# Channel attention in a four-layer model: buffers cleared in front, GpSimd in written order, keys split from queries and made a batch earlier

## The chip, the core and the metric

The kernel runs on one core of one Trainium2 chip. The metric is device time in microseconds (us) of one execution; lower is better. Engines are called as the profile calls them: PE (TensorE matmuls), PEld (its weight loads), DVE (VectorE), ACT (ScalarE), POOL (GpSimd) and SP (SyncE, which here only issues DMAs). "L1567" is line 1567 of the kernel before the change.

## The reference

The model has four layers, each with an attention over a context and a feed-forward part, both gated by a `tanh`. The activations `x` are 16 batches of 128 x 256 in f32, the context `c` likewise. The change concerns the attention of the last layer, which runs over channels: the 128 rows are 16 heads of 8 channels, and the 256 columns are the positions.

```python
q = jnp.einsum('oc,bct->bot', Wq, x) + bq[None, :, None]      # x is layernormed over its columns
k = jnp.einsum('oc,bct->bot', Wk, c) + bk[None, :, None]
v = jnp.einsum('oc,bct->bot', Wv, c) + bv[None, :, None]
q, k, v = (t.reshape(B, 16, 8, -1) for t in (q, k, v))
scores = jnp.einsum('bhkt,bhks->bhts', q, k) * SCALE
p = jax.nn.softmax(scores, axis=-1)
out = jnp.einsum('bhts,bhks->bhkt', p, v).reshape(B, 128, T)
return jnp.einsum('oc,bct->bot', Wo, out) + bo[None, :, None]
# and around it:  x = x + tanh(g) * attention(layernorm(x), c)
```

Ahead of it stands a mixture of experts, whose rows lie sorted in DRAM (`ys`); its sum into `x` is made by this stage. After it comes a last feed-forward stage.

## The kernel before, in words

The whole pass is one program; the stage in question is `stage_l3x`. It runs without the search for row maxima (`search` is false in the pass that is timed; a second pass with `search` runs only if a flag demands it).

**The work of one batch `b`.** `begin` fetches the two expert rows of every token with two indirect DMAs issued by POOL (`fetch`, L709, tile `yc`, three buffers) and loads the context (`cb`) through SP. `stats` adds the two rows into `x` with their weights (L1524), takes mean and variance (L1527 to L1530). `rsqrt` raises the variance to -0.5 on POOL (L1535). `normal` writes the normalised queries `xn` on DVE (L1541). `project` makes queries (L1553, from `xn`) and keys (L1554, from `cb`) in one PSUM tile `qk`; `biased` adds the biases on DVE (tile `f`, L1559 and L1560). `halves` splits `f` into a rounded half (ACT, L1566) and the rest (POOL, L1567) in one tile `hl` for queries and keys together, and SP writes them in four DMAs to a DRAM scratch `scr` (L1571, L1573), one scratch per buffer set. `spread` reads the scratch back in four DMAs (L1589) into `qa` and `ka`, where a head has its rows on the partitions that the score matmuls want. `project_v` and `keep_v` make the values in `v`.

**Scores and products.** The loop runs over units `n = 8 b + u`. In each unit `weigh` makes one score group of four matmuls on PE (`s`, L1660, two PSUM buffers) and one exponential on ACT (`pt`, L1667). Two units feed one value product of 16 matmuls (`values`, `av`, L1676), which DVE copies out (`keep_values`, `avs`, L1687). When the four products of a batch are there, `back` transposes them (`ta`, L1692), `normalise` divides, `turn` transposes again (`tt`), `output` projects (`y`), `store` scales on ACT (`ys`, L1723) and adds to `x` on POOL (L1725).

**What sets the order.** PE, DVE and ACT are under a manual schedule: they execute in the order in which the code writes the instructions. That order is two tables: `taken[u]` lists what is written before score group `u`, `made[u]` what is written after it, each with the number of batches it runs ahead. POOL and SP are ordered by the framework's scheduler, which placed eight gathers at the head of POOL's stage and from then on a pair after each `hl`. There are three sets of `qa`, `ka` and `v` (`NB = 3`); `clear` sets a set to zero when its first batch comes: `qa` on DVE (L1546), `ka` and `v` on ACT (L1548), and a column of `v` to one on POOL (L1549).

Of the kernel before, what the change touches and what calls it, by code (L numbers as in the profile page):

```python
# [10 lines left out]
F32 = mybir.dt.float32  # L11
BF16 = mybir.dt.bfloat16
F32R = mybir.dt.float32r
AF = mybir.ActivationFunctionType
ALU = mybir.AluOpType
# [3 lines left out]
P = 128  # L19
B = 16  # L20
D = 256
# [34 lines left out]
def passage(ctx: ExitStack, tc: tile.TileContext, a: dict, out: bass.AP, inv, flag):  # L56
    nc = tc.nc
    search = inv is None
# [60 lines left out]
    ones = cst.tile([P, P], F32, name="ones")  # L119
# [46 lines left out]
    def bc(ap, axis, n):  # L166

        u = ap.unsqueeze(axis)
        shape = list(u.shape)
        shape[axis] = n  # L170
        return u.to_broadcast(shape)
# [1306 lines left out]
    def stage_l3x(wn, bn, wv, won, bov, pos, wgt, ys):  # L1478
# [5 lines left out]
        SC = float(1.0 / np.sqrt(8))  # L1484
        LEAD = 12
        NB = 4 if search else 3
        with tc.tile_pool(name="l3", bufs=1) as l3, tc.tile_pool(name="l3w", bufs=2) as w_, tc.tile_pool(
            name="l3d", bufs=1, space=bass.MemoryType.DRAM
# [3 lines left out]
            engines={mybir.EngineType.PE, mybir.EngineType.DVE, mybir.EngineType.Activation}  # L1492
# [3 lines left out]
            scr = [l3d.tile([8, P, D], F32, name=f"scr{i}") for i in range(NB)]  # L1496
            zr = l3.tile([2, P], F32, name="zr")
# [6 lines left out]
            def begin(b):  # L1504
                fetch(b)
                cbs[b] = w_.tile([P, D], F32, name="cb", bufs=3 if search else 4)
                nc.sync.dma_start(cbs[b], a["ctx"][b])
# [43 lines left out]
            def project(b):  # L1551
                ps["f", b] = t = psa.tile([P, 2, D], F32, name="qk", tag="a")
                nc.tensor.matmul(t[:, 0, :], lhsT=wn[0], rhs=xns.pop(b), start=True, stop=True)  # L1553
                nc.tensor.matmul(t[:, 1, :], lhsT=wn[1], rhs=cbs[b], start=True, stop=True)  # L1554

            def biased(b):
                t = ps.pop(("f", b))
                fs[b] = f = w_.tile([P, 2, D], F32, name="f")
                nc.vector.tensor_scalar(f[:, 0, :], t[:, 0, :], bn[0], SC, ALU.add, ALU.mult)  # L1559
                nc.vector.tensor_scalar(f[:, 1, :], t[:, 1, :], bn[1], None, ALU.add)  # L1560

            def halves(b):

                f = fs.pop(b)
                hl = w_.tile([P, 2, 2, D], F32R, name="hl")
                nc.scalar.copy(hl[:, :, 0, :], f)  # L1566
                nc.gpsimd.tensor_tensor(hl[:, :, 1, :], f, hl[:, :, 0, :].bitcast(F32), ALU.subtract)  # L1567
                s = scr[b % NB]
                hf = hl.bitcast(F32)
                for x in range(2):  # L1570
                    nc.sync.dma_start(s[2 * x : 2 * x + 2].rearrange("s p t -> p s t"), bc(hf[:, 0, x], 1, 2))  # L1571
                for x in range(2):
                    nc.sync.dma_start(s[4 + 2 * x : 6 + 2 * x].rearrange("s p t -> p s t"), hf[:, 1])  # L1573

            def spread(b):

                s = scr[b % NB]
                for h in range(2):
                    r = slice(64 * h + 32, 64 * h + 34)
                    if not search:  # L1580
                        continue
                    if b < NB:
                        nc.sync.dma_start(kas[b][r].bitcast(F32), bc(ones[0:2, :], 1, 16))
                    else:
                        nc.sync.dma_start(qas[b % NB][r].bitcast(F32), bc(zr, 1, 16))
                s = s.rearrange("s (k h) t -> (s k) (h t)", h=16)
                for h in range(2):
                    for x, t in enumerate((qas, kas)):
                        nc.sync.dma_start(  # L1589
                            t[b % NB][64 * h : 64 * h + 32].bitcast(F32).rearrange("p j t -> p (j t)"),  # L1590
                            s[32 * x : 32 * x + 32, 2048 * h : 2048 * h + 2048],
                        )
# [140 lines left out]
            if search:  # L1733
# [3 lines left out]
                    ((keep_values, -1, 3), (biased, 4)),  # L1737
                    ((normalise, -1, 0), (halves, 4), (keep_v, 3)),
# [7 lines left out]
                    ((values, -1, 3), (project, 4)),  # L1746
# [5 lines left out]
                    ((values, 0, 2), (output, -1), (spread, 4)),  # L1752
                )
            else:
                taken = (
                    ((begin, 4), (rsqrt, 3), (keep_values, -1, 2), (spread, 2)),
                    ((normal, 3), (clear, 3)),
                    ((keep_values, -1, 3),),
                    ((normalise, -1, 0), (normalise, -1, 1), (biased, 3)),
                    ((keep_values, 0, 0), (halves, 3)),  # L1760
# [5 lines left out]
                    (),  # L1766
                    ((values, -1, 3),),
                    ((back, -1, 0), (back, -1, 1), (project, 3)),
# [5 lines left out]
                )  # L1774
            for n in range(-40, 8 * B + 17):
                b, u = divmod(n, 8)
                for f, d, *r in taken[u]:
                    when(f, b + d, *r)
                if search and 0 <= n + LEAD < 8 * B:
                    top(n + LEAD)  # L1780
                if 0 <= n < 8 * B:
                    weigh(n)
                for f, d, *r in made[u]:
                    when(f, b + d, *r)
# [280 lines left out]
```

## Time and profile before

| | |
|---|---|
| median of 3 runs | 1079.16 us (1078.13 to 1082.75) |
| the profiled execution | 1077.04 us, of which span 1075.3 us |
| busy in the span | PE 904.1, PEld 602.5, DVE 607.5, ACT 456.8, POOL 342.3 us |
| the stage `stage_l3x` | from about 752 us (first clear on ACT at 752.50) to about 970 us of the span |
| first score group of the stage | 786.87 us |
| last score matmul starts | 968.7 us |
| score groups, `s`, L1660 | 512 matmuls, 64.3 us busy |
| exponentials, `pt`, L1667 | 128 instructions of 1024 ns |
| value products, `av`, L1676 | 1024 matmuls, 69.4 us busy |
| halves on POOL, `hl`, L1567 | 16 instructions of 1282 ns |

The page's busy times are sums over stages with different limits. Times in the stage are counted from the start of the span. A bracket at the end of a line of the timeline tells how long the engine stood idle before the line, and what it is thought to have waited for.

### The profile page before, as it was taken

The page shows a single profiled execution, that of the slowest core. Times are in us where ns is not written, and L with a number is a line of the kernel's source. Part 1 is how long each engine was busy: PE and PEld are TensorE (multiplying, and loading weights), DVE is VectorE, ACT ScalarE, POOL GpSimd, SP SyncE. Part 2 cuts the span into 40 slices and gives each one's busy share as a digit, 9 for nine tenths or more (in the row PEclk, how much of TensorE's full clock was granted, in tenths as well). Part 3 has the DMA queues.
Part 4 walks back from the last instruction along what each step waited for, and adds up shares of the span by engine and source line. Part 5 has one row for each costly group of instructions (what it writes and reads, how often), then busy time and mean ns, then how long its engine had stood idle before and what let it go on. Part 6 is the DMA issues. An engine that isn't in the chain of part 4 may idle for free. (4 is left out here: it accounts for less than half of the span.)

```text
span 1075.3 us, 14892 instructions
## 1 busy us (share of the span) xinstructions
PE 904.1 (84%) x5212; PEld 602.5 (56%) x5212; DVE 607.5 (56%) x1537; ACT 456.8 (42%) x707; POOL 342.3 (32%) x389
## 2 busy tenths in 40 slices
PE   3899978899999888888864858998169999998797
PEld 1444456677778444455443747887145555555564
DVE  5988966322225656787788586454345555534442
ACT  1211024223322446666762242454257777882111
POOL 5766322543115324211111046550443342201000
PEclk9999979999999978999986557899579999997999
DMA  9100070233341109800000202352488887530000
GB/s 305 41 1 1 0 220 21 63 104 109 69 143 50 39 20 144 78 1 1 1 1 1 78 1 88 109 145 82 142 247 235 220 222 195 164 79 1 20 30 32
DMA packets 71401, 94.12 MB, mean 88 GB/s; under 512 B 9271, under 2 KB 63127, under 8 KB 69015
## 3 DMA queue, kind: packets, MB, share of 16 engines
q1 hardware_dynamic: 56952, 67.21, 21.1%
q0 software_dynamic: 14080, 23.78, 11.4%
q10 hardware_dynamic: 288, 2.10, 0.5%
q8 instruction: 45, 0.74, 0.3%
q14 instruction: 36, 0.29, 0.1%
HBM read 57.06 MB, written 33.55 MB: 84 GB/s over the span
## 5 line engine op out<-in xcount | busy, mean ns | idle before, releaser
L1667 ACT ACTIVATE pt<-s 128x1024 f32<-128x1024 f32 x128 | 126.4, 1024 | 32.5 <-PE s L1660 29.8
L709 POOL DMA_INDIRECT yc<-ys,pos x64 | 62.4, 975 | 125.0 <-DVE x L729 49.2
L297 PE MATMUL y<-kv,toep 128*128 128x512 f32 x192 | 86.6, 602 | 1.6 <-DVE toep L237 1.6
L1660 PE MATMUL s<-qa,ka 64*128 64x256 f32 x512 | 64.3, 332 | 8.3 <-ACT pt L1667 7.5
L1676 PE MATMUL av<-pt,v 128*32 128x256 f32 x1024 | 69.4, 389 | 0.1
L289 POOL TENSOR_TENSOR kv<-ctxT 128x1024 f32<-128x1024 f32 x32 | 60.2, 1900 | 28.3 <-PE y L297 28.3
L1660 PEld LDWEIGHTS s<-qa,ka 64*128 64x128 f32 x512 | 38.6, 188 | 46.9 <-issue 23.2
L1687 DVE COPY avs<-av 128x256 f32<-128x256 f32 x64 | 27.1, 423 | 65.5 <-PE av L1676 48.5
L297 PEld LDWEIGHTS y<-kv,toep 128*128 128x128 f32 x192 | 35.6, 192 | 43.7 <-issue 40.3
L616 PE MATMUL ub<-L0we,xbT 128*128 x160 | 50.8, 460 | 2.6 <-ACT xbT L607 2.6
L593 POOL DMA_INDIRECT xb<-xs,who x40 | 38.2, 954 | 43.3 <-PE tb L605 33.2
L913 PE MATMUL yb<-L2we,hT 88*128 (+1 forms) x224 | 41.7, 315 | 9.6 <-DVE hT L737 3.9
L848 POOL DMA_INDIRECT xb<-xs,who x40 | 38.1, 953 | 31.7 <-PE tb L860 20.9
L302 DVE TENSOR_TENSOR pr<-y,qT 128x1024 f32<-128x1024 f32 x32 | 39.0, 1222 | 12.1 <-PE y L297 9.4
L1567 POOL TENSOR_TENSOR hl<-f,hl 128x512 fp32r<-128x512 f32 x16 | 20.5, 1282 | 79.5 <-ACT hl L1566 79.5
L477 PE MATMUL up<-L0s,xT 128*128 128x352 f32 x128 | 43.0, 482 | 0.0
L913 PEld LDWEIGHTS yb<-L2we,hT 88*128 88x128 f32 x224 | 33.6, 205 | 16.5 <-DVE hT L737 9.0
L1086 PE MATMUL s<-qa,ka 18*128 18x512 f32 x128 | 37.4, 660 | 4.9 <-ACT follow L1380 4.9
L305 DVE TENSOR_REDUCE oT<-pr 128x128 f32<-128x1024 f32 x32 | 38.9, 1219 | 1.0
L1676 PEld LDWEIGHTS av<-pt,v 128*32 128x32 f32 x1024 | 26.9, 110 | 20.4 <-issue 0.7
L642 PE MATMUL yb<-L0we,hTb 88*128 x160 | 37.9, 379 | 0.0
L616 PEld LDWEIGHTS ub<-L0we,xbT 128*128 128x128 f32 x160 | 28.8, 190 | 15.5 <-ACT xbT L607 2.8
(384 smaller groups left out, 2043.1 us busy)
## 6 DMA issues: line engine op xcount, KB each, us to landing
scr<-hl SPq DMA_DIRECT2D x64, 256.0 KB
ys<-ysb SPq DMA_DIRECT2D x40, 256.0 KB
qa<-scr SPq DMA_DIRECT2D x32, 256.0 KB
ka<-scr SPq DMA_DIRECT2D x32, 256.0 KB
L2we<-in_L_w_dram POOLq DMA_DIRECT2D x6, 792.0 KB
L0we<-in_L_w_dram SPq DMA_DIRECT2D x6, 704.0 KB
xs<-xn SPq DMA_DIRECT2D x8, 512.0 KB
x<-in_x_dram SPq DMA_DIRECT2D x4, 512.0 KB
```

Of the source, the lines that this page charges most:

```text
L289: nc.gpsimd.tensor_tensor(t, bc(ch, 3, 8), bc(ch, 2, 8), ALU.mult)
L297: nc.tensor.matmul(y[:, ns], lhsT=T[:, h, d : d + P], rhs=kv[mc][:, ns], start=(mc == 0), stop=(mc == lc))
L302: nc.vector.tensor_tensor(pr, y.rearrange("p (b j i) -> p b j i", b=B, j=8), bc(qT[:, lc, :, hs], 2, 8), ALU.mult)
L305: nc.vector.tensor_reduce(oT[:, lc, :, hs], pr, AX.X, ALU.add)
L477: nc.tensor.matmul(t[:, n, 0 : 2 * I], lhsT=xT[:, c, b * P : (b + 1) * P], rhs=s13[:, c, n, :], start=(c == 0), stop=(c == 1),)
L593: nc.gpsimd.indirect_dma_start(out=xbs[s][:, i, :], out_offset=None, in_=xs, in_offset=bass.IndirectOffsetOnAxis(ap=who[:, 2 * s + i : 2 * ...
L616: nc.tensor.matmul(t[:, i, 0 : 2 * I], lhsT=xbT[:, i, c, :], rhs=we[:, bass.ds(regs[s][i] + c * 2 * I, 2 * I)], start=(c == 0), stop=(c == 1),
L709: nc.gpsimd.indirect_dma_start(out=got[b][:, i, :], out_offset=None, in_=ys, in_offset=bass.IndirectOffsetOnAxis(ap=pos[:, i, b : b + 1], ...
L913: nc.tensor.matmul(y[:, i, :], lhsT=hT[:, x, k, i, :], rhs=we[0:HI, bass.ds(at[i] + 4 * I + k * D, D)], start=(n == 0), stop=(n == 3),)
L1660: nc.tensor.matmul(s[:, h, jj, :], lhsT=ka[r, 2 * i + jj, sc * P : (sc + 1) * P], rhs=qa[r, 2 * i + jj, :], start=True, stop=True,)
L1667: nc.scalar.activation(pts[b, i][:, sc], s, AF.Exp)
L1676: nc.tensor.matmul(av[c : c + 32, :], lhsT=va[:, sc, 8 * h + 2 * i + jj, :], rhs=pt[:, sc, h, jj, :], start=(sc == 0), stop=(sc == 1),)
```

## The change

It does four things in `stage_l3x`, all for the pass without search as far as order goes.

1. POOL joins the manual schedule of the stage, so its instructions stand in written order.
2. All three sets of buffers are cleared before the loop, not one by one in it.
3. `project`, `biased`, `halves` and `spread` take queries (`x = 0`) and keys (`x = 1`) separately, with tiles of half the size: `qk` and `f` hold one of them, `hl` has four buffers of half size. The number of scratches is `NB + 1 = 4`.
4. Keys are projected, split and written to scratch a batch earlier than queries. The keys of the first three batches are also spread at once (`ahead`); those of later batches are spread with the queries of the same batch (`behind`). The context is loaded five batches ahead; the gathers (`fetch`, four ahead) now stand after the `rsqrt` of their unit.

```diff
-            engines={mybir.EngineType.PE, mybir.EngineType.DVE, mybir.EngineType.Activation}
+            engines={
+                mybir.EngineType.PE, mybir.EngineType.DVE,
+                mybir.EngineType.Activation, mybir.EngineType.Pool,
+            }
...
-            scr = [l3d.tile([8, P, D], F32, name=f"scr{i}") for i in range(NB)]
+            NS3 = NB + 1
+            scr = [l3d.tile([8, P, D], F32, name=f"scr{i}") for i in range(NS3)]
...
+            def project(b, x):
+                ps["f", b, x] = t = psa.tile([P, D], F32, name="qk", tag="a")
+                nc.tensor.matmul(t, lhsT=wn[x], rhs=cbs[b] if x else xns.pop(b), start=True, stop=True)
...
+            def halves(b, x):
+                f = fs.pop((b, x))
+                hl = w_.tile([P, 2, D], F32R, name="hl", bufs=4)
+                nc.scalar.copy(hl[:, 0, :], f)
+                nc.gpsimd.tensor_tensor(hl[:, 1, :], f, hl[:, 0, :].bitcast(F32), ALU.subtract)
+                s = scr[b % NS3]
+                hf = hl.bitcast(F32)
+                for i in range(2):
+                    at = 4 * x + 2 * i
+                    nc.sync.dma_start(
+                        s[at : at + 2].rearrange("s p t -> p s t"), hf if x else bc(hf[:, i], 1, 2)
+                    )
...
+            def ahead(b):
+                if b < NB:
+                    spread(b, 1)
+
+            def behind(b):
+                if b >= NB:
+                    spread(b, 1)
+                spread(b, 0)
...
                 taken = (
-                    ((begin, 4), (rsqrt, 3), (keep_values, -1, 2), (spread, 2)),
-                    ((normal, 3), (clear, 3)),
-                    ((keep_values, -1, 3),),
-                    ((normalise, -1, 0), (normalise, -1, 1), (biased, 3)),
-                    ((keep_values, 0, 0), (halves, 3)),
+                    ((context, 5), (rsqrt, 3), (fetch, 4), (keep_values, -1, 2), (behind, 2)),
+                    ((normal, 3), (biased, 4, 1)),
+                    ((keep_values, -1, 3), (halves, 4, 1)),
+                    ((normalise, -1, 0), (normalise, -1, 1), (biased, 3, 0), (ahead, 4)),
+                    ((keep_values, 0, 0), (halves, 3, 0)),
...
                 made = (
-                    (),
+                    ((project, 4, 1),),
                     ((values, -1, 3),),
-                    ((back, -1, 0), (back, -1, 1), (project, 3)),
+                    ((back, -1, 0), (back, -1, 1), (project, 3, 0)),
...
+                for b in range(NB):
+                    clear(b)
             for n in range(-40, 8 * B + 17):
```

## The prediction

> **What bounds the kernel now.** I read the table by stretches first, over the channel attention (752 to 970 us of the span); columns are span, then busy us and instructions of PE, PEld, DVE, ACT and POOL, then granted clock, DMA share and GB/s.
>
> ```profile
> 752.00:770.00 18.00, 2.04 (x4) 1.17 (x4) 4.91 (x10) 3.38 (x4) 8.55 (x11) 0.50 0.35 102
> 770.00:787.00 17.00, 5.92 (x18) 4.68 (x18) 9.19 (x19) 6.98 (x7) 7.86 (x10) 0.50 0.75 216
> 787.00:798.00 11.00, 6.70 (x44) 3.92 (x44) 3.42 (x10) 6.56 (x8) 4.72 (x5) 0.67 0.87 241
> ...
> 813.20:824.90 11.70, 11.14 (x120) 6.58 (x116) 6.45 (x22) 9.06 (x12) 4.51 (x6) 1.00 0.98 289
> ...
> 907.05:918.18 11.13, 11.07 (x122) 6.58 (x118) 6.33 (x22) 9.18 (x12) 2.54 (x4) 1.00 0.75 202
> ```
>
> There are two regimes. Up to 798 no engine is full: PE works 14.7 of 46 us, at half clock. This is the ramp, a chain of waits. After it PE is busy 11.1 of every 11.1 to 11.7 us: a plateau that PE bounds. The ramp's waits come next (total us, times, longest):
>
> ```profile
> PE qk L1553 <- DVE xn L1541: 28.8, 4, 15.0
> DVE xn L1541 <- POOL rs L1535: 10.0, 3, 3.3
> ```
>
> PE waits for the normalised queries, and those wait for GpSimd's power. GpSimd's timeline says why:
>
> ```profile
> 756.03 0.95 POOL L709 DMA_INDIRECT yc<-ys,pos  x1 [3.83 <-ACT v L1548]
> ...
> 764.80 0.95 POOL L709 DMA_INDIRECT yc<-ys,pos  x1 [0.30 <-issue]
> 765.77 0.60 POOL L1535 TENSOR_TENSOR rs<-ve,neghalf 128x1 f32<-128x1 f32 x1
> 770.65 1.27 POOL L1567 TENSOR_TENSOR hl<-f,hl 128x512 fp32r<-128x512 f32 x1 [4.28 <-ACT hl L1566]
> 772.08 1.00 POOL L709 DMA_INDIRECT yc<-ys,pos  x1 [0.16 <-issue]
> 773.39 0.95 POOL L709 DMA_INDIRECT yc<-ys,pos  x1 [0.30 <-issue]
> 774.36 0.59 POOL L1535 TENSOR_TENSOR rs<-ve,neghalf 128x1 f32<-128x1 f32 x1
> ```
>
> The variance of batch 0 was ready at 761.77, but eight gathers stood ahead of the power: 4.0 us lost. Later powers stand behind two gathers each. DVE writes xn at 766.40, 774.99, 783.54 and 792.18, about 8.6 us apart; the fourth is the last obstacle, because the projection of batch 3 stands in PE's order before score group 3 of batch 0 (794.65), and from there the plateau runs.
>
> The plateau itself changes pace: 11.73 us a batch up to 907, 11.12 after. The last gather is issued at 895.23. In a batch with gathers:
>
> ```profile
> 824.82 0.95 POOL L709 DMA_INDIRECT yc<-ys,pos  x1 [0.30 <-issue]
> 824.90 1.06 PE L1660 MATMUL s<-qa,ka 64*128 64x256 f32 x8
> 825.80 0.58 POOL L1535 TENSOR_TENSOR rs<-ve,neghalf 128x1 f32<-128x1 f32 x1
> 826.30 0.42 DVE L1687 COPY avs<-av 128x256 f32<-128x256 f32 x1 [2.19 <-PE s L1660]
> 826.42 2.85 ACT L1667 ACTIVATE pt<-s 128x1024 f32<-128x1024 f32 x3 [1.01 <-PE s L1660]
> ```
>
> Score group 0 ends at 825.40, yet ACT takes it 1.01 us later and DVE takes the value product that ended at 824.97 1.33 us later. In the batches after 907 these two lags are 0.10 and 0.07. So a pair of gathers holds up the news of PE's results, about 0.6 us a batch in nine batches.
>
> **The change part by part.** I work against the profiled execution, 1077.04 us (1.74 around its 1075.3 span); the median of runs, 1079.16, lies 2.12 above, so I add the difference to the median. What one measurement can tell apart is about 0.5%, 5.4 us.
>
> *Clears in front.* ACT clears a key and a value buffer in 2.85 us (752.50 to 755.35); three sets end near 761.05. GpSimd's three small memsets are now written before the first gather and wait for ACT's value clears, so the first gather moves from 756.03 to about 761.35: a loss of 5.3 us at the head. The sum there: its variance came 5.74 us after the first gather's start, so now at 767.1; power 0.60; xn(0) near 767.8 against 766.40, 1.4 us late. DVE's memsets (3 x 1.77 us from 752) end at 757.3, under the wait for data, and leave the chain, where one stood after each early xn. If that cover went, each would cost 1.8.
>
> *GpSimd in written order.* The power now stands ahead of the next gathers, but the next batch's gathers come only after it. One step is therefore power 0.60, gap 0.16, then 5.74 from gather to variance: 6.5 us. That 5.74 was measured with idle queues; here scratch traffic runs beside it. The queue's longest wait for a scratch write was 5.1 us against a mean of 1.5 (29.2 over 20), so a delay of 0 to 1.4 a step is the bound: 6.5 to 7.9, and I take 7.1, since two of the three steps meet spreads. xn(3) then falls at 767.8 + 3 x 7.1 = 789.1 (787.3 to 791.5) against 792.18.
>
> *Keys apart.* Before score group 3 only the query projection is left behind xn(3): 0.46 plus 1.22 = 1.7 us against 2.47 (792.18 to 794.65), 0.8 less. The ramp gains 3.1 + 0.8 = 3.9 us (1.5 to 5.7). Keys of the first three batches need only the context; scratch writes and spreads for them run at 764 to 780, where DMA was 0.35 to 0.75 busy. SP's order puts the spread of queries 0 behind the write of keys 2, which waits for GpSimd near 777.5; with 4.4 us for two spreads (packets of the first, 776.4 to 780.9, all four) it lands near 783.5, just under PE's own readiness at 784.4. Another microsecond late there costs the same at group 0 but not at group 3. Each half copy (ACT 0.37 by the 128x256 value copy, GpSimd about 0.65 by half of 1.28) adds some 0.1 us of ACT per batch, beside 2 us of idle.
>
> *The plateau.* PE's work is unchanged: 2 x 0.44 us of projection, now one after group 0 and one after the transposes. Gathers still run in twelve batches, now after the power, which stands behind the store's add (ACT's ys ends 824.49, add 0.73, power 0.58): gathers near 825.9 and 827.2 on the clock of the batch shown, 2.4 us later. Group 0 is then read at once. The results near the pair are now the value product -1,3 (ends near 827.3) and group 2 (827.7). DVE's copy of the former stands before PE's transposes, which follow at 827.7. If the news comes 0.7 us late (over the nine batches DVE showed two lags, 0.66 three times and 1.3 six times) the copy ends at 828.5 and PE loses about 0.5: as much as now. I take an unchanged 11.73, plus two more batches with gathers (2 x 0.6). From both sides: 9 x 0.6 = 5.4 gained if no lag falls on the path; 8.4 lost if the lag is 1.3 (rival 2).
>
> Here a page differs from the rows. The Trainium skill, SBUF — State Buffer, Who interferes with whom, says that only DVE and GpSimd share a port pair and that PE and ACT never wait on anyone. By it ACT's lag would not be GpSimd's, the place and number of the gathers would cost nothing, and the sum would be the ramp's -3.9 alone, 1075.3. The rows, 1.01 us with gathers against 0.10 without, speak against that, and I go by them.
>
> Sum: -3.9 + 1.2 = -2.7 us; 1079.16 - 2.7 = **1076.5**, and this case's own range is 1074 to 1080.
>
> **Rivals.** 1. *The lag disappears from the path:* the key projection fills the slot in which PE waited (0.55 us at group 2) and the gathers hit results that nobody needs soon. For it: batches from 907 run at 11.12. Against: gathers stay. Nine batches gain 0.6: -3.9 - 5.4 = -9.3, 1070 us (1067.5 to 1072).
>
> 2. *The lag moves onto the transposes, slower than before.* If DVE learns of product -1,3 at 828.65 (1.3 us late, as in six of nine batches now), its copy ends at 829.1 and PE stands 1.25 us over the 11.12 pace: 9 x 0.64 + 2 x 1.25 = +8.3, less the ramp's 3.9: +4.4, 1083.6; with the ramp at its low end +6.8, 1086. It decides from a lag above 1.0 us on that copy; below 0.7 it is my case.
>
> 3. *The ramp does not get shorter:* gathers on the critical chain, beside spreads, need 8.6 us a step or more, and the late head is not won back: ramp +1, plateau +1.2, 1081.4. Against: the empty-queue row leaves 2 us a step.
>
> The clock is a smaller matter: 0.50 until 787 in the rows. The Trainium skill, TensorE: Matmul & The Clock Gate, What's actually happening, has full clock return after about 3.4 us of sustained work; keys spread thinly over the ramp would by that rule not bring it back, and the sum stays. Did the clock rise earlier, the first two value products alone (1.93 us at half clock, 1.07 at full) would take the sum from -2.7 to -4.4.
>
> **How the numbers follow.** Forecast 0.43, rival 1 0.27, rival 2 0.22, rival 3 0.08. Faster by over 0.5%: rival 1 and a sliver of the forecast, 0.29. Slower: the upper half of rival 2, a little of rival 3 and of what I have not seen, 0.17. Same: 0.54. Range 1067 to 1086 takes in rival 1 and nearly all of rival 2.
>
> **What would show it.** In the changed profile: first gather near 761.4 and three memsets before it; powers ahead of gathers, xn near 767.8, 775, 782, 789; score group 0 near 784.5 and group 3 near 791; a batch near 11.7 with ACT's lag at group 0 gone and DVE's copy of product -1,3 late by 0.7. Wrong if xn's step is over 8, if the first scores wait for qa or ka, or if a batch runs at 11.1 (rival 1) or 12.3 (rival 2).

## Result and the profile after

The changed kernel takes 1077.9 us (median of 18 runs) against 1080.03 for the kernel before beside it; the ratio is 0.9984 (95% interval 0.9971 to 0.9998), so about 1.7 us less. A second measurement, in the third set below, gave 0.9998 (0.9972 to 1.0023), so the gain is small enough that one of two measurements doesn't see it. The forecast of 2.7 us less, within what one measurement can tell from no change, held; two of its terms did not.

The profiled execution took 1079.52 us with a span of 1077.7, which is 2.4 us *longer* than the one before. ACT's first clear starts 3.66 us later in it (756.16 against 752.50), and nothing that lies ahead of that clear was changed. So I count from that clear. The work is cut in two stretches: **R**, the ramp, from ACT's wait just ahead of its first clear (0.46 us before the clear starts in every profile) to score group 0 of batch 1; and **P**, the plateau, from there to score group 0 of batch 15. Before: R 49.4, P 158.8. After: R 47.9, P 158.6. The sum falls by 1.7 us, as the measured ratio does.

The table by stretches (columns as before; the limits are those of the prediction's table, though the stage begins 3.66 us later here):

```profile
752.00:770.00 18.00, 4.54 (x19) 3.02 (x18) 7.06 (x7) 10.18 (x10) 3.29 (x7) 0.60 0.25 76
770.00:787.00 17.00, 5.93 (x16) 4.02 (x17) 8.91 (x22) 2.29 (x6) 9.42 (x13) 0.60 0.71 209
787.00:798.00 11.00, 6.94 (x32) 4.07 (x35) 3.57 (x9) 5.83 (x8) 5.47 (x7) 0.50 1.03 294
...
813.20:824.90 11.70, 11.51 (x119) 6.56 (x118) 6.53 (x23) 9.36 (x12) 4.67 (x6) 1.00 0.84 237
907.05:918.18 11.13, 10.92 (x116) 6.32 (x116) 5.98 (x22) 8.90 (x12) 4.67 (x6) 1.00 0.81 225
```

The clears stand in the first row (8.3 us of ACT's 10.18). The third row is new: the DMA engines are full (1.03 against 0.87; with the limits moved by 3.66 us, 1.08). What the ramp waits for (total us, times, longest):

```profile
PE qk L1564 <- DVE xn L1551: 18.5, 4, 9.4
DVE x L1534 <- DMA yc<-ys,pos: 14.4, 6, 5.7
PE qk L1564 <- DMA cb<-in_ctx_dram: 7.5, 2, 5.7
```

PE's wait for the queries fell from 28.8 to 18.5 us, and the long waits of xn for GpSimd's power are gone from the head of the list. DVE's wait for gathered rows took their place: once 9.9 us before, six times 14.4 in all now. The line of before:

```profile
DVE x L1524 <- DMA yc<-ys,pos: 9.9, 1, 9.9
```

PE waits for a context as well, and its first scores wait for `qa`:

```profile
788.90 0.55 PE L1679 MATMUL s<-qa,ka 64*128 64x256 f32 x1 [1.13 <-DMA qa<-scr]
...
792.41 1.19 PE L1564 MATMUL qk<-cb,l3kn 128*128 128x256 f32 x2 [1.79 <-DMA cb<-in_ctx_dram]
...
795.51 1.22 PE L1564 MATMUL qk<-xn,l3qn 128*128 128x256 f32 x2 [0.76 <-DVE xn L1551]
```

GpSimd's timeline:

```profile
764.55 0.15 POOL L1559 MEMSET v<- 128x32 f32 x1 [2.59 <-ACT v L1558]
765.98 0.95 POOL L709 DMA_INDIRECT yc<-ys,pos  x1 [1.27 <-issue]
...
771.57 0.58 POOL L1545 TENSOR_TENSOR rs<-ve,neghalf 128x1 f32<-128x1 f32 x1 [2.64 <-DVE ve L1540]
...
785.69 1.00 POOL L709 DMA_INDIRECT yc<-ys,pos  x1 [0.18 <-issue]
...
794.38 0.57 POOL L1545 TENSOR_TENSOR rs<-ve,neghalf 128x1 f32<-128x1 f32 x1 [5.00 <-DVE ve L1540]
```

The first gather stands behind three memsets, and then behind 1.27 us of nothing that the profile shows. Each power now comes as soon as its variance is there, and the gathers follow it. From the gather at 785.69 to the end of the variance at 794.29 it takes 8.6 us, where the idle queue took 5.74. The DMA queues (packets, MB, share) show why; first in the stretch from 785.7 to 790, then from 790 to 792.2:

```profile
q1 hardware_dynamic: 550, 1.07, 97.9%
```
```profile
q1 hardware_dynamic: 557, 0.66, 85.0%
q0 software_dynamic: 96, 0.26, 29.8%
```

q0 carries the gathers. In the first 4.3 us after its issue the pair moved no packet at all; q1, with the spreads of batch 0 and then the scratch writes, held 98% of the engines. The pair's first packet came at 790.79, 5.1 us after the gather's start; with idle queues it was 1.7 us (gather at 765.98, packet at 767.64). So the steps of xn are 7.08, 6.28 and 9.44 us (16.0, 23.1, 29.4 and 38.8 us after the first clear), against 8.6 each before (13.9 to 39.7).

On the plateau, in a batch with gathers:

```profile
816.82 1.00 POOL L709 DMA_INDIRECT yc<-ys,pos  x1 [0.18 <-issue]
817.21 1.07 PE L1695 MATMUL av<-pt,v 128*32 128x256 f32 x16
...
818.90 0.42 DVE L1706 COPY avs<-av 128x256 f32<-128x256 f32 x1 [1.37 <-PE s L1679]
...
819.38 0.77 PE L1711 MATMUL ta<-ident,avs 128*128 128x128 f32 x5 [0.19 <-issue]
819.71 1.02 ACT L1686 ACTIVATE pt<-s 128x1024 f32<-128x1024 f32 x1 [1.06 <-PE ta L1711]
```

The value product (-1,3) ends at 818.28 and DVE copies it at 818.90, 0.62 us late; PE's transposes stop after three of eight for want of that copy. ACT reads group 2 (ended 818.71) 1.00 us late. Group 0 is read after 0.10. Batches 2 to 9 take 11.60 us (median) against 11.73; batches 10 and 11, which had no gathers before, also take 11.61 now.

### The profile page after: what moved, and what is told of

The parts are those of the page before. It is cut to its first block, busy times and chain, and to the rows that moved or that the text cites. A ratio compares the mean times of both kernels' runs of the same rounds, so it can differ in the third digit from the quotient of the medians.

```text
span 1077.7 us, 14988 instructions
## 1 busy us (share of the span) xinstructions
PE 910.5 (84%) x5212; PEld 600.9 (56%) x5212; DVE 609.0 (57%) x1537; ACT 460.4 (43%) x723; POOL 344.4 (32%) x405
## 5 line engine op out<-in xcount | busy, mean ns | idle before, releaser
L1679 PEld LDWEIGHTS s<-qa,ka 64*128 64x128 f32 x512 | 39.5, 190 | 41.9 <-issue 27.8
L297 PEld LDWEIGHTS y<-kv,toep 128*128 128x128 f32 x192 | 35.6, 192 | 44.1 <-issue 40.7
L913 PE MATMUL yb<-L2we,hT 88*128 (+1 forms) x224 | 41.4, 312 | 10.5 <-ACT hT L736 5.3
L848 POOL DMA_INDIRECT xb<-xs,who x40 | 38.0, 950 | 33.7 <-PE tb L860 22.8
L305 DVE TENSOR_REDUCE oT<-pr 128x128 f32<-128x1024 f32 x32 | 38.9, 1220 | 1.0
L1044 PE MATMUL tq<-xT,l1q 128*128 128x256 f32 x128 | 35.8, 429 | 2.4 <-ACT xT L1035 2.4
L616 PEld LDWEIGHTS ub<-L0we,xbT 128*128 128x128 f32 x160 | 28.8, 190 | 15.7 <-ACT xbT L607 3.0
```

The source lines that it names most:

```text
L297: nc.tensor.matmul(y[:, ns], lhsT=T[:, h, d : d + P], rhs=kv[mc][:, ns], start=(mc == 0), stop=(mc == lc))
L305: nc.vector.tensor_reduce(oT[:, lc, :, hs], pr, AX.X, ALU.add)
L616: nc.tensor.matmul(t[:, i, 0 : 2 * I], lhsT=xbT[:, i, c, :], rhs=we[:, bass.ds(regs[s][i] + c * 2 * I, 2 * I)], start=(c == 0), stop=(c == 1),
L913: nc.tensor.matmul(y[:, i, :], lhsT=hT[:, x, k, i, :], rhs=we[0:HI, bass.ds(at[i] + 4 * I + k * D, D)], start=(n == 0), stop=(n == 3),)
L1679: nc.tensor.matmul(s[:, h, jj, :], lhsT=ka[r, 2 * i + jj, sc * P : (sc + 1) * P], rhs=qa[r, 2 * i + jj, :], start=True, stop=True,)
```

## The experiments

Three sets of four kernels ran on three chips. The chips matter: the kernel before takes 1076.8, 1063.5 and 1076.9 us on them. Ratios are to the kernel before on the same chip. All stretches are worked out from the profiles' timelines; "group 3" is score group 3 of batch 0, counted like xn from ACT's first clear, "gather" is the start of a batch's first gather counted from score group 0, and "batch" is the median of batches 2 to 9.

| kernel | set | xn(0), xn(3) | group 3 | R | P | gather | batch | ratio (95%) |
|---|---|---|---|---|---|---|---|---|
| before | first | 13.9, 39.7 | 42.2 | 49.4 | 158.8 | -1.38 | 11.73 | |
| after | first | 16.0, 38.8 | 40.5 | 47.9 | 158.6 | +1.10 | 11.60 | 0.9984 (0.9971-0.9998) |
| clears back in loop | 1 | 10.0, 34.4 | 37.5 | 45.1 | 158.0 | +1.10 | 11.54 | 0.9970 (0.9953-0.9987) |
| GpSimd scheduled | 1 | 14.0, 34.5 | 39.0 | 45.8 | 154.4 | -1.38 | 11.26 | 0.9935 (0.9912-0.9958) |
| keys beside queries | 1 | 16.0, 38.9 | 41.4 | 47.7 | 155.8 | +1.10 | 11.26 | 0.9968 (0.9954-0.9982) |
| no plateau gathers | 1 | 15.9, 39.1 | 40.7 | 48.5 | 153.7 | none | 11.19 | 0.9949 (0.9930-0.9969) |
| keys alone | 2 | 14.5, 37.8 | 41.4 | 47.4 | 153.9 | -1.38 | 11.19 | 0.9991 (0.9971-1.0011) |
| order alone | 2 | 10.0, 33.7 | 36.2 | 42.7 | 154.0 | +1.10 | 11.12 | 0.9944 (0.9928-0.9960) |
| gathers ahead | 2 | 10.0, 27.7 | 36.1 | 42.7 | 153.7 | +1.10 | 11.19 | 0.9956 (0.9939-0.9973) |
| keys, six contexts | 2 | 14.8, 38.1 | 39.7 | 46.3 | 153.9 | -1.38 | 11.19 | 0.9975 (0.9962-0.9988) |
| before again | 3 | 13.9, 39.7 | 42.1 | 49.5 | 158.8 | -1.38 | 11.72 | |
| after again | 3 | 16.0, 39.2 | 40.9 | 48.7 | 158.1 | +1.10 | 11.56 | 0.9998 (0.9972-1.0023) |
| clears alone | 3 | 13.9, 39.6 | 42.1 | 49.5 | 158.5 | -1.38 | 11.72 | 1.0008 (0.9989-1.0028) |
| combined | 3 | 10.4, 27.7 | 34.4 | 41.9 | 166.9 | +0.56 | 12.58 | 1.0003 (0.9980-1.0025) |

**Clears back in the loop** (the changed kernel with one part undone).

```
-                    ((normal, 3), (biased, 4, 1)),
+                    ((normal, 3), (clear, 4), (biased, 4, 1)),
...
-                for b in range(NB):
-                    clear(b)
```

> The changed kernel with its clears put back into the loop, one batch at a time, each just ahead of that batch's first use; GpSimd's order is still written out and the keys still run ahead, so the first pair of gathers now stands before all three small memsets. Counted from ACT's first clear of a key buffer (756.16 in the changed kernel's profile, where the first gather follows 9.8 us later, xn(0) 16.0 us later and score group 3 of batch 0 40.5 us later). Theory A, the clears in front delay the chain by holding the first gather: first gather at most 3.5 us after that clear, xn(0) near 11 to 13, steps between xn as in the changed kernel (7.1, 6.3, 9.4), group 3 near 36 to 37; batch 11.6 as it was; time 3.5 to 4.5 us below the changed kernel's, about 1074. Theory B, the ramp is set by the traffic of spreads and scratch writes and not by the head: group 3 within 1 us of 40.5 and the time within 1 us of 1077.9. Theory C, the clears cost more between the steps (1.8 us of DVE and 5.7 us of ACT for each batch) than in front: xn's steps of 9 us or more, group 3 later than 41.5, time above 1079.

The first gather came 3.53 us after the first clear (9.82 in the changed kernel), xn(0) at 10.0 and group 3 at 37.5 instead of 40.5; R fell by 2.8. Theory A, though group 3 is 0.5 us later than its range, the first step took 8.4 us instead of 7.1, and the time fell short of it: 0.9970 against the changed kernel's 0.9984 is 1.5 us, where 3.5 to 4.5 were expected. (ACT's two clears of a batch take 2.85 us, not theory C's 5.7.) With GpSimd's order written, clears in front cost the ramp about 3 us.

**GpSimd left to the scheduler** (the second part undone).

```
                 mybir.EngineType.Activation,
-                mybir.EngineType.Pool,
```

> The changed kernel with GpSimd taken out of the written order; clears in front and keys apart stay. The scheduler then puts three pairs of gathers ahead of the first power and lets every later power stand behind a pair of gathers, two batches ahead of their use. Theory A, the written order's steps carry the gather's latency and the scheduler's do not: xn(0) later than the 16.0 us after ACT's first clear that the changed kernel shows, but steps of 4 to 6 us in place of 7.1, 6.3 and 9.4, group 3 of batch 0 near 33 to 38 us after the first clear (40.5 in the changed kernel); on the plateau the lag returns to ACT's read of score group 0 and a batch takes 11.7 instead of 11.59, in about two batches fewer with gathers. Sum about -3 + 1.2 - 0.9, so 1074 to 1076. Theory B, the prediction's reasoning: the scheduler's order costs 8.6 us a step as in the kernel before, so group 3 comes 2 to 4 us later than in the changed kernel, and the time is 1080 to 1083.

The ramp goes theory A's way, a shorter one, without its numbers: xn(0) at 14.0 and not later than 16.0, steps of 7.25, 6.84 and 6.38, group 3 at 39.0, R 2.1 below the changed kernel. The plateau refutes both theories: ACT's lag at group 0 came back (1.03 us in batch 6), yet a batch took 11.26 us. In the kernel before the same gathers at the same place (-1.38) cost 11.73. The difference between the two is the key projection, which now stands between groups 0 and 1 and gives PE work while ACT is late: PE's pause ahead of group 2 is 0.05 us in batch 6, and 0.56 in the kernel before. This is the fastest kernel of its set, 0.9935.

**Keys beside the queries** (the third part undone).

```
-                    ((context, 5), (rsqrt, 3), (fetch, 4), (keep_values, -1, 2), (behind, 2)),
+                    ((context, 4), (rsqrt, 3), (fetch, 4), (keep_values, -1, 2), (behind, 2)),
-                    ((normal, 3), (biased, 4, 1)),
+                    ((normal, 3),),
...
-                    ((normalise, -1, 0), (normalise, -1, 1), (biased, 3, 0), (ahead, 4)),
-                    ((keep_values, 0, 0), (halves, 3, 0)),
+                    ((normalise, -1, 0), (normalise, -1, 1), (biased, 3, 0), (biased, 3, 1)),
+                    ((keep_values, 0, 0), (halves, 3, 0), (halves, 3, 1)),
...
-                    ((back, -1, 0), (back, -1, 1), (project, 3, 0)),
+                    ((back, -1, 0), (back, -1, 1), (project, 3, 0), (project, 3, 1)),
```

> The changed kernel with the keys of a batch projected, copied, written and spread beside its queries again, no longer a batch ahead; the halves stay apart as two operations each, clears in front and GpSimd's written order stay. Theory A, the keys' lead is worth what the prediction gave it: score group 3 of batch 0 comes about 0.8 us later relative to xn(3), 41 to 42 us after ACT's first clear of a key buffer instead of 40.5; batch 11.6; time about 1 us above the changed kernel's. Theory B, the lead also takes the spread of the keys out of the wait before the first scores: score group 0 waits for four spreads of about 1.1 us each instead of two, comes 2 us or more later than the 32.7 us after the first clear in the changed kernel, and the time is 2 to 4 us higher. Theory C, keys ahead are what loads the queue while the gathers of the third step land (9.4 us): without them that step falls to 7 us, group 3 comes 1 us or more earlier and the time falls by 1 to 2 us.

Group 3 came 0.9 us later (41.4), as the prediction's 0.8 has it, and group 0 2.9 us later (35.6). The third step did fall to 6.6 us, but the second rose to 10.0: the slow step moved to where the first spreads now run, so theory C is out. The surprise is again the plateau, and it makes the kernel faster than the changed one where theories A and B had it slower: 11.26 us a batch with the gathers at +1.10. Without the key projection between groups 0 and 1 the product (-1,3) ends 0.96 us after the pair's start (847.78 against 846.82) and not 1.46; DVE's copy is 0.36 us late instead of 0.62, and PE's eight transposes run through. With the clears in front, the keys apart and the written order each bring 11.73 to 11.26; together they give 11.60.

**No gathers on the plateau.**

```
-            fetch = fetcher(w_, ys, pos, 3)
+            fetch_ = fetcher(w_, ys, pos, 4)
+
+            def fetch(b):
+                return fetch_(b % 4)
```

> The changed kernel without the gathers of batches 4 to 15, which add the rows gathered for batches 0 to 3 a second, third and fourth time instead (this part of the computation is left out; nothing else is). Theory A, a pair of indirect gathers on GpSimd delays the news of PE's results and that alone separates a batch of 11.59 us from one of 11.12: all batches from the third on take 11.1, DVE's copy of the value product (-1,3) lags 0.07 us everywhere and ACT reads group 2 at once; time lower by 9 or 10 x 0.47, about 1073.4. Theory B, GpSimd's other work (powers, subtractions, adds) or the plain transfers of the scratch delay it: batches stay at 11.5 to 11.6 up to the last with transfers and the time stays within 1 us of 1077.9. The ramp is as in the changed kernel in both.

Theory A: 11.19 us in batches 2 to 11, DVE's copy of product (-1,3) 0.07 us late, ACT's read of group 2 0.10. From group 2 to group 3 PE takes 1.89 us here and 2.30 with the gathers. That 0.41 is the whole price of a pair in the changed kernel. The powers, subtractions and scratch transfers all ran.

**Keys alone** (the kernel before with one part of the change; the same edit as the two undone parts above together).

> The kernel before with the keys apart and ahead as the only part of the change: clears in the loop, GpSimd's order left to the scheduler. Two stretches are compared in every profile: R, from ACT's first clear of a key buffer to score group 0 of batch 1 (49.4 us in the kernel before, 47.9 in the changed one, 45.1 with the clears in the loop, 45.8 with GpSimd scheduled), and P, from there to score group 0 of batch 15 (158.8, 158.6, 158.0 and 154.5). Theory A, keys apart take the late read of score group 0 off the path as long as the gathers stay where the scheduler puts them, and the other two parts only take from that: batch 11.25 with ACT's lag of about 1 us at group 0 still there, P near 154.5; R near 45; time 0.993 of before or lower. Theory B, the clears in front are needed for the shorter ramp: R 48 or more, time 0.996. Theory C, the 11.25 of the run with GpSimd scheduled comes from the clears' place and not from the keys: batch 11.7, P 158.5, time 0.999.

R is 47.4, nearer to theory B's 48 than to A's 45. P of 153.9 looks like theory A's, but the reason isn't A's: ACT read group 0 after 0.10 us although the gathers ran at -1.38. None of this set's profiles shows late news, so the set says nothing on what the keys do against it.

**Order alone** (the kernel before with GpSimd's written order: the edit of the keys beside, and the clears in the loop).

> The kernel before with GpSimd's written order as the only part of the change: clears in the loop, keys projected and spread beside their queries (the halves still go as two operations of each engine). R and P as in the run with the keys alone. Theory A, both keys apart and the written order move the gathers' late news away from ACT's read of score group 0, and each alone gives 11.25 us a batch; only both together put it on the transposes at full length: batch 11.25 here, P near 155.8 as in the run with keys beside; R 45 to 47.5, the clears costing 1.8 us of DVE in some steps; time 0.994 to 0.997 of before. Theory B, the written order is bad by itself: batch 11.6 or more, P above 158, time 0.999 or more.

R is 42.7, 6.7 us below the kernel before of the other sets, the most of any single part and more than either theory had; xn(0) at 10.0, steps of 6.76, 9.99 and 6.90. The written order isn't bad by itself. A batch takes 11.12, every result read within 0.1 us or as soon as its reader is free.

**Gathers ahead of the clears and a batch earlier** (on the changed kernel).

```
+                fetch(0)
+                fetch(1)
                 for b in range(NB):
                     clear(b)
...
-                    ((context, 5), (rsqrt, 3), (fetch, 4), (keep_values, -1, 2), (behind, 2)),
+                    ((context, 5), (rsqrt, 3), (fetch, 5), (keep_values, -1, 2), (behind, 2)),
```

> The changed kernel with the first two pairs of gathers ahead of the three clears and every later pair written one batch earlier; GpSimd's order stays written, the pair stays just behind a power. Theory A, the ramp of the changed kernel is a chain of power, gather and variance, with the gather's landing (3.9 us idle, 6.3 beside spreads) in each step: without it first gather about 4 us after ACT's first clear in place of 9.8, xn(0) at 10 to 11 in place of 16, steps of 4.5 to 6 us in place of 7.1, 6.3 and 9.4; the spreads of the first queries and the context of batch 4 then come last, R falls from 47.9 to 40 to 44; P stays near 158 (a pair of gathers fewer, batch 11.6); time 4 to 7 us below the changed kernel's, 0.992 to 0.995 of before. Theory B, DMA traffic sets the ramp whatever the gathers' place: xn early, but score group 0 not before 30 and R not below 45; time 0.996 or more.

Theory A: the steps are 5.91, 5.90 and 5.90 us, xn(3) comes at 27.7 instead of 38.8. DVE's adds start the moment it is their turn (the line is the second of the two), and another wait is last:

```profile
755.35 1.51 DVE L1534 SCALAR_TENSOR_TENSOR x<-yc,wgt,x 128x256 f32<-128x256 f32 x1
```
```profile
775.16 1.19 PE L1564 MATMUL qk<-cb,l3kn 128*128 128x256 f32 x2 [2.19 <-DMA cb<-in_ctx_dram]
```

The add of 1.51 us runs beside POOL's subtractions (754.92 to 756.57); with POOL free of them, at 750.40, it takes 0.48. So each pair of adds takes 2.10 us and not 1.00, and about 1.1 us of each 5.9 us step may be this overlap.

xn(3) is 11.1 us earlier and R only 5.2: score group 0 still waits for its spread (28.7), and between groups 0 and 1 PE waits 2.19 us for the context of batch 4. On the plateau the instructions stand as in the changed kernel, but the chip is another:

```profile
830.61 0.99 POOL L709 DMA_INDIRECT yc<-ys,pos  x1 [0.18 <-issue]
831.01 1.07 PE L1695 MATMUL av<-pt,v 128*32 128x256 f32 x16
...
832.15 0.42 DVE L1706 COPY avs<-av 128x256 f32<-128x256 f32 x1 [0.82 <-PE av L1695]
```

The product starts 0.40 us after the gather, as in the changed kernel (0.39), ends at 832.08 and is read 0.07 us later, not 0.62. A batch takes 11.19, so P isn't near theory A's 158, and the ratio, 0.9956, lies just above its range.

**Six context buffers** (on the kernel with the keys alone).

```
-                cbs[b] = w_.tile([P, D], F32, name="cb", bufs=3 if search else 4)
+                cbs[b] = w_.tile([P, D], F32, name="cb", bufs=3 if search else 6)
```

> As the run with the keys alone, with six context buffers instead of four, so that the context of batch 4 need not wait until the value projection of batch 0 has let a buffer go. Theory A, PE's wait for the context of batch 4 between score groups 0 and 1 of batch 0 (1.8 us in the changed kernel's profile, 2.2 with GpSimd scheduled) sets when group 3 comes where the queries of batch 3 are early: R 1 to 2 us shorter than with the keys alone, P the same; time 1 to 2 us lower. Theory B, the wait only covers for the spread or the queries of batch 3: group 3 and R unchanged within 0.5 us.

Group 1 follows group 0 after 2.3 us instead of 4.6, group 3 comes 1.7 us earlier and R falls by 1.1: theory A, at its lower end.

**The two kernels again, on one chip** (no edit).

> The kernel before, unchanged, for its profile beside those of this set. In the profiles of the first set the news of PE's results came up to 1.35 us late near a pair of gathers; in the second set, on another chip with the same kernels running 13 us faster, DVE and ACT read every result 0.07 to 0.10 us after its end although the gathers ran. Theory A, the late news belongs to the chip and not to the kernel: whichever this chip is, all four kernels of this set show it or none does; with it a batch of this kernel takes 11.73 us and ACT reads score group 0 about 1 us late, without it 11.12 and 0.10, and P (score group 0 of batch 1 to that of batch 15) is 158.8 or 153.3. Theory B, it comes and goes with the kernel: this one shows it everywhere, 11.73. R (ACT's first clear of a key buffer to score group 0 of batch 1) 49.4 in both.

> The changed kernel, unchanged, on the chip of this set. R 47.9 as before. If the late news belongs to the chip and this one has it: batch 11.59, the copy of product (-1,3) 0.6 us late, P 158.6, ratio 0.998. If this chip doesn't have it: batch 11.19, P 154 against 153.3 for the kernel before, ratio 0.999; the whole effect of the change is then its ramp.

This chip has the late news in all four profiles: 1.00 us at ACT's read of group 0 and 11.72 us a batch before, 0.55 us at DVE's copy and 11.56 after. That is theory A as far as sets of one chip can show it. R came 0.8 us above the first profile of the changed kernel; half of it stands ahead of group 3 (third step 9.65 instead of 9.44).

**Clears alone** (the kernel before with only the clears in front).

```
-                    ((normal, 3), (clear, 3)),
+                    ((normal, 3),),
...
+            for b in range(0 if search else NB):
+                clear(b)
```

> The kernel before with the clears in front as the only part of the change. Theory A, each step between xn loses the 1.8 us of DVE's clear that stood in it: xn(0) about 14.4 us after ACT's first clear as before, steps of 6.8 instead of 8.6 us, xn(3) near 35 instead of 40.1, R 44.5 to 46 against 49.4; P as in the kernel before; ratio 0.996 to 0.997. Theory B, the prediction's head: gathers or the first power wait for the clears, xn(0) near 16, R 47 or more, ratio 0.998 or above.

Neither theory: xn(0) at 13.9, steps of 8.58, 8.54 and 8.63, R 49.5, nothing moved at all. The step is a chain that DVE's clear was never part of. From xn at 767.71 on:

```profile
768.22 1.19 PE L1553 MATMUL qk<-xn,l3qn 128*128 128x256 f32 x2 [14.97 <-DVE xn L1541]
...
770.30 0.48 DVE L1559 TENSOR_SCALAR f<-qk,l3bq 128x256 f32<-128x256 f32 x1 [2.19 <-PE qk L1554]
...
771.96 1.26 POOL L1567 TENSOR_TENSOR hl<-f,hl 128x512 fp32r<-128x512 f32 x1 [4.18 <-ACT hl L1566]
773.38 1.00 POOL L709 DMA_INDIRECT yc<-ys,pos  x1 [0.16 <-issue]
774.68 0.95 POOL L709 DMA_INDIRECT yc<-ys,pos  x1 [0.30 <-issue]
775.65 0.60 POOL L1535 TENSOR_TENSOR rs<-ve,neghalf 128x1 f32<-128x1 f32 x1
```

In the scheduler's order the power of the next batch stands behind the subtraction of this one, which waits for PE, DVE and ACT, and then behind the gathers. The variance had been ready since 772.96. That is what the written order takes away.

**The parts that paid, together.**

```
-            fetch = fetcher(w_, ys, pos, 3)
+            fetch = fetcher(w_, ys, pos, 2)
...
-                cbs[b] = w_.tile([P, D], F32, name="cb", bufs=3 if search else 4)
+                cbs[b] = w_.tile([P, D], F32, name="cb", bufs=3 if search else 6)
...
+            def early(b):
+                if b < 4:
+                    rsqrt(b)
+
+            def late(b):
+                if b >= 4:
+                    rsqrt(b)
...
-                    ((context, 5), (rsqrt, 3), (fetch, 4), (keep_values, -1, 2), (behind, 2)),
+                    ((context, 5), (late, 3), (keep_values, -1, 2), (behind, 2)),
...
-                    ((store, -1), (stats, 4)),
+                    ((store, -1), (stats, 4), (early, 4), (fetch, 6)),
...
+                fetch(0)
+                fetch(1)
```

> The parts that paid, together: the changed kernel with the first two pairs of gathers ahead of the clears, later pairs written right behind the variance two batches ahead (in the ramp behind that batch's power, from batch 4 on ahead of it, so that they start where DVE's add lets a buffer go, as the scheduler placed them), two gather buffers and six context buffers. If the costs add as the runs so far have them: xn(0) 10.5 us after ACT's first clear, steps near 6, xn(3) near 28.5; no wait for the context of batch 4; score group 0 near 29 and group 3 near 34; R 40 to 41 against 49.4 before and 47.9 after; batch 11.19 on a chip without late news, 11.25 on one with it; ratio 0.991 without, 0.988 with it. Rival: the scratch traffic holds group 0 at 29 and the spreads of batch 1 hold its first scores, R stays at 42.7 as with the gathers ahead alone; ratio 0.994 or 0.991.

The ramp is the shortest, 41.9, and group 3 comes at 34.4. The plateau lost it all: 12.58 us a batch, P 8.1 us above before. The gathers did not land where the scheduler had them. In my written order they stand behind the store's add, so they start 0.56 us after group 0 and not 1.38 before it; and the power stands behind them:

```profile
840.27 0.99 POOL L709 DMA_INDIRECT yc<-ys,pos  x1 [0.16 <-DVE avs L1714]
...
841.21 1.07 PE L1703 MATMUL av<-pt,v 128*32 128x256 f32 x16
...
842.53 0.59 POOL L1545 TENSOR_TENSOR rs<-ve,neghalf 128x1 f32<-128x1 f32 x1
...
843.16 0.41 DVE L1559 TENSOR_SCALAR xn<-x,mv,rs 128x256 f32<-128x256 f32 x1 [2.88 <-POOL rs L1545]
843.49 0.48 DVE L1578 TENSOR_SCALAR f<-qk,l3bk 128x256 f32<-128x256 f32 x1
843.88 0.41 DVE L1714 COPY avs<-av 128x256 f32<-128x256 f32 x1
...
844.35 0.77 PE L1719 MATMUL ta<-ident,avs 128*128 128x128 f32 x5 [1.16 <-DVE avs L1714]
```

The product ends at 842.28, DVE copies it at 843.88, 1.60 us late, and PE stands 1.16 us in its transposes. Less than half of that is late news: PE's semaphore event for the product is on record at 843.03, 0.75 us late. DVE wasn't free for it then. Its written order puts xn and a bias ahead of the copy; xn waited 2.88 us for the power, which stood behind the pair of gathers, and the copy follows without a pause. So most of the delay comes from a power behind gathers, the fault of the kernel before, and the prediction's second rival, a copy held up by late news alone, isn't shown here.

## Why the prediction held, and where it was wrong

**The ramp, the term of -3.9 us, was mis-sized: R fell by 1.47 (0.9 in the second profile) and group 3 came 1.65 us earlier, at or below the low end of the range I gave it (1.5 to 5.7).** Two of the signs that I had set for being wrong came: a step of xn over 8 us (9.44), and first scores that wait for `qa` (1.13 us). Four things went into it.

*The head.* Predicted from the first clear: first gather at 8.85 us, xn(0) at 15.3. Measured: 9.82 and 16.0. I allowed nothing between the last memset and the first gather; it was 1.27 us.

*The step.* I took 7.1 us for each and at most 7.9, from an idle gather plus 0 to 1.4 us of queue. Two steps were 7.08 and 6.28, the third 9.44. The 1.4 was the mean wait of a scratch write before; that row also had a longest of 5.1, and the pair that meets the spreads waits like the longest: no packet for over 4 us. xn(3) came at 38.8 instead of the predicted 36.6. The run with the gathers ahead shows that the gather's landing is that chain: without it the steps are 5.9 us each. Here the Trainium skill, Perfetto Trace Analysis, DMA Instruction — SWDGE (GPSIMD), bears on the reading: an indirect DMA's record ends with its descriptors and not with its data. The trace agrees: the pair's records end at 787.95, its packets move after 790.

*A second path.* I put the context of batch 4 at nothing. PE waited 1.79 us for it ahead of group 1 and was ready for the queries of batch 3 only 0.76 us before they came. So, as an estimate from these rows, xn(3) at the predicted 36.6 would have brought group 3 forward by 0.76 us and not by 2.2.

*The keys.* Group 3 follows xn(3) after 1.68 us; predicted 1.7. But the gain did not reach R: from group 3 to batch 1 the changed kernel takes 7.0 us and the one with keys beside 5.8, so the two have the same ramp (47.9 and 47.7). Those 1.2 us are the clock. PE doesn't pause in that stretch in any of the fourteen profiles, and its length follows the granted clock: 5.50 us at 1.00 (keys alone), 5.79 at 0.94 (keys beside), 6.98 at 0.75 here and 7.35 at 0.70 in the changed kernel's second profile. So R carries up to 1.9 us that depend on when the clock comes back, and group 3 tells the parts apart better.

*The clock.* I called it the smaller matter, and between these two kernels it was: it came back for good 44.0 us after the first clear, against 45.2 before. My sum for an earlier return was too large: only the first value product of the kernel before ran at half clock (1.93 us, the second 1.07), so 0.86 us and not 1.7 stood to gain. It takes 1.93 in the changed kernel too.

**One statement was wrong without a number on it.** I wrote that DVE's memsets leave the chain, where one stood after each early xn. The clears alone move nothing: they lay beside PE's projections all along.

**The plateau was right in its mechanism and nearly in size.** Predicted: group 0 read at once, the copy of product (-1,3) 0.7 us late, PE losing 0.5, a batch of 11.73, two more batches with gathers. Measured: 0.10, 0.62, 0.41, 11.60, and the gathers run to batch 11. P moved by -0.2 instead of +1.2: eight batches gained 0.13 each, where I had no gain, and batches 10 and 11 lost 0.96, where I had 1.2; batch 1 lost 0.34 and batch 12 gained 0.43 (10.69 against 11.12), because no key projection is left for it. I had neither of the last two.

So the sum of -1.7 comes close to the predicted -2.7 with two errors that partly cancel, +2.4 in the ramp and -1.4 on the plateau. That the total came so near is luck in part.

**The rivals.** The first (the lag leaves the path) is what the keys apart do as long as the scheduler places the gathers: 11.26 with the lag of 1.03 still there. I set against it that the gathers stay; it is that the written order moves them. The second decides from a lag above 1.0 us on the copy, I said; the changed kernel has 0.62. The combined one has 1.60 and 12.58 us a batch, but mostly from DVE's order, so no run shows this rival. The third needed steps of 8.6 or more; one of three was.

**The parts do not add up.** R by parts: none 49.4, clears 49.5, keys 47.4, order 42.7, clears and keys 45.8, order and keys 45.1, clears and order 47.7, all three 47.9. By group 3, which the clock touches less: none 42.2, clears 42.1, keys 41.4, order 36.2, clears and keys 39.0, order and keys 37.5, clears and order 41.4, all three 40.5. The written order alone takes 6.0 us off group 3; adding the clears in front gives 5.3 of them back, because their memsets then hold the first gather (9.82 us after the first clear instead of 3.53), and adding the keys gives back 1.3. The profiles are of different chips; two profiles of the changed kernel on two occasions differ by 0.4 us in group 3.

The kernel before is beaten: by clears and keys with GpSimd scheduled (0.9935 on a chip with late news), and by the written order alone (0.9944 on a chip without). The two were not run on the same chip, and the changed kernel not beside either; its own ratio is 0.9984.

## What to carry to other kernels

A gather on GpSimd has two prices, and both depend on its place to half a microsecond: its rows come late when it is issued together with a megabyte of other transfers, so it belongs a step ahead of the chain that needs it; and the results of PE that end near it may be read late, so nothing that PE waits for should end there. Writing an engine's order out by hand fixes both, for better or worse: look at what its first instruction waits for, at what each instruction lands on, and at who waits for what you put behind a gather. A long delay next to a known cause may still have another: in the combined kernel DVE simply wasn't free. When a change has several parts, run each alone: here one part was worth 6.0 us of the ramp and the others took most of it back.

## What the runs showed of the hardware

**Late news of PE's results near an indirect DMA, on some chips.** With a pair of gathers running, DVE, idle and waiting, reads results that had ended up to 1.36 us before; without gathers the same reads come after 0.07 to 0.10 us. PE's ends are modelled, but the semaphore events on record show the same: in the kernel before, three results that end at 824.97, 825.40 and 825.96 are reported together, at 826.27, 826.33 and 826.39, while PE goes on with its next matmuls. Only PE's reports are held: in the changed kernel the product that ends at 818.28 is reported at 818.88, and ACT's exponential that ends at 818.35 at 818.36. In the second set, on another chip, the same gathers at the same places had no such effect, and batches took 11.12 to 11.19 us. Three pairs of kernels have the same order on the plateau and differ in the set: after and gathers ahead (11.60 and 11.19), keys beside and order alone (11.26 and 11.12), GpSimd scheduled and keys alone (11.26 and 11.19). Sums agree with it: if the kernel before has 11.12 us in its gather batches there and the R of the other sets, R + P is 202.7, and the four kernels of that set should gain 1.4, 6.0, 6.3 and 2.6 us; the ratios give 1.0, 6.0, 4.7 and 2.7. The Trainium skill, SBUF — State Buffer, Who interferes with whom, says that PE and ACT never wait on anyone. It speaks of ports of that memory; here it is the report of a finished matmul that comes late, and no run shows whether a port has to do with it. Whether the chip is the cause, and which part of it delays the news, stays open: three sets are few, and the kernel before was not profiled on the second chip. Nor is the recording ruled out: in the second set's profiles every semaphore event of PE is on record, in the others 10 to 27 of about 1050 are missing.

**Queues are not shared evenly in time.** For 4.3 us the queue of the gathers moved nothing while the other, with packets of spreads and scratch writes, held 98% of the DMA engines; 1.7 us of that also pass with idle queues.

**How long PE takes follows the granted clock, and when that comes back varies.** The same instructions, from group 3 to batch 1, take 5.50 us at a granted clock of 1.00 and 7.35 at 0.70, without a pause of PE in either.
